# Gathers of a graph network layer: one completion semaphore for each pair of groups

## The chip, the cores and the metric

The kernel runs on one core of a Trainium2 chip. The metric is the device time of one execution in microseconds (us). Several executions are timed, and one further execution is recorded by the hardware profiler.

The engines have these names here: PE multiplies matrices (PEld is its loading of weights), DVE works on vectors, ACT applies functions, POOL is the engine that issues gathers, and SP issues plain transfers. PSUM is the memory that PE writes its results to. Engines tell each other of finished work by semaphores: counters that one raises and others wait on.

## What is computed

The layer works on 12500 nodes with 96 channels and 412500 edges with 4 attributes, sorted by target node `dst`. Cut to what matters:

```python
def mlp(h, W, b, gamma, beta):          # mean and var over all rows
    h = relu(h @ W + b)
    return gamma * (h - mean(h)) * rsqrt(var(h) + 1e-5) + beta

node = mlp(x, W_node, ...)
edge = mlp(edge_attr, W_edge, ...)
message = mlp(concatenate([x[src], x[dst], edge], axis=1), W_msg, ...)
y = x + segment_sum(message, dst) + node
out = layernorm(y)
```

The part that costs is the message of each of the 412500 edges, which needs the row `x[src]` (96 floats, 384 bytes) of an arbitrary node.

## The kernel before

**Units.** 128 edges are a tile, 4 tiles a group (512 edges), 4 groups a block. There are 3223 tiles, 806 groups and 202 blocks.

**Tables.** The product of `x` with the first part of `W_msg` is computed once for each node and put into a table `p_tab` in DRAM (`tables`, L146 to L166); the part for `dst` goes into `q_tab`. The message of an edge is then the row `src` of `p_tab`, plus a small matrix product of its edge attributes and a window of `q_tab`.

**Gathers.** `gather` (L168 to L175) fetches the rows of one group: four indirect transfers, issued by POOL at L172, each of 128 rows. The group's rows land in one tile of SBUF.

**Spilled blocks.** While the tables, the node part (`nodes`, L254 to L284) and the edge statistics (`edge_norm`, L286 to L338) run, POOL already gathers the first 26 blocks ("early" blocks). `blocks` (L177 to L184) gathers 16 tiles into a buffer `stage` (two of these) and SP stores it to DRAM as `spill`. The first three of them gather from `x` itself, since the table isn't there yet. In `edge_norm`, PE L303 multiplies, ACT L307 applies relu, and DVE L309 takes statistics; four PSUM buffers lie between PE and ACT.

**The ring.** Then 21 buffers, each for one group, form a ring (`ring`, tiles named `pg`). POOL fills all 21 (84 gathers) before the main loop.

**The main loop** (in `fast`, L522 to L545) goes over the groups in a fixed order: the 176 late blocks, fetched through the ring, with one early block after every six or seven of them, read back from `spill` as `pb` by SP. For each group k:

- `linear(k + 1)`: PE L464 computes `z` of the next group, four matmuls into one of two PSUM buffers.
- `message(k)`: DVE L475 adds `z` and the gathered rows into `hs`. On a block's third group DVE L478 also builds the places of the targets. On its last group ACT L482 applies relu to all of `hs`, giving `h`.
- `sums(k - 4)`: PE L497 sums `h` of the group before by target node, into `pa`.
- `edges` and `prepare`: once a block, PE L450 and ACT L457 make the next block's edge features `left` by way of `pr`.
- `add`: once a block, DVE L510 and L511 add the sums to `agg` and the second moments to `gram`.
- `load` and `fetch`: once a block, SP loads edge attributes (L408, L410) and the window of `q_tab` (L418) for the block after next.
- `ahead_of`: after each group that came from the ring, POOL issues the four gathers of the group 21 further on, into the buffer that this group's `hs` has just given free.

**What sets the order.** `manual_schedule` keeps the instructions of SP and POOL in the order in which the program writes them from the start, and those of all five engines in the main loop. No scheduler moves anything there.

**Who waits for what.** The framework puts in the waits. It has eight semaphores for POOL's gathers and deals them out in turn. A gather may only be issued when the gather that used the same semaphore last, the one eight before, has landed. The first gather of a group waits, besides, for the DVE instruction that set its buffer free. `hs` at L475 waits for the four gathers of its group, for PE's `z`, and once a block for ACT. An instruction holds one wait of its own; further waits are put ahead of it as separate instructions on the same engine that do nothing else.

Of the kernel before, what the change touches and what calls it, by code (L numbers as in the profile page):

```python
# [26 lines left out]
GT, GE, BG = 4, 512, 4  # L27
NT = -(-E // P)
NG = -(-NT // GT)
# [22 lines left out]
SPILL = 26 * BG  # L52
# [4 lines left out]
CL, CE = 2, 2  # L57
BUSY = 4
J = 8


K, W, ROWS = 4, 128, 12672
# [11 lines left out]
def gnn(ctx, tc, t):  # L74
    nc = tc.nc
# [70 lines left out]
    def tables(work, ps):  # L146
# [3 lines left out]
        for c in range(0, NB, CH):  # L150
# [14 lines left out]
                (nc.scalar if (c // CH + k) % 2 else nc.sync).dma_start(outs[k][:, c:c + CH, :], r[:, :, k, :])  # L165
            yield  # L166

    def gather(g, pg):  # L168
        tab, idx = (t["x"], src_raw) if g < RAW * BG else (p_tab, src)
        for i in range(min(GT, NT - g * GT)):  # L170
            k = g * GT + i
            nc.gpsimd.indirect_dma_start(  # L172
                out=pg[:, i, :], out_offset=None, in_=tab[:, :],
                in_offset=bass.IndirectOffsetOnAxis(ap=idx[:, k:k + 1], axis=0))
        return pg  # L175

    def blocks():  # L177

        for b in range(SPILL // BG):
            pg = ring.tile([P, BG, GT, C], F32, name="stage", bufs=2)  # L180
            for i in range(BG):
                gather(b * BG + i, pg[:, i, :, :])
            nc.sync.dma_start(spill[b], pg.rearrange("p g a c -> p g (a c)"))
            yield  # L184
# [15 lines left out]
    for i in range(NS):  # L200
        k, n = Q * i, C - Q * i
# [84 lines left out]
    def edge_norm():  # L286

        with tc.tile_pool(name="es", bufs=2) as work, tc.tile_pool(name="es1", bufs=1) as one, \
                tc.tile_pool(name="es_ps", bufs=4, space=PSUM) as ps:
            stats = one.tile([P, NS, NBL, 6], F32, name="estats")  # L290
            for b in range(NBL):
                if b % J == 0:
                    yield
                    ea = work.tile([P, J, GE], F32, name="ea")
                    n = min(J, NBL - b)
                    for i in range(NS):
                        nc.sync.dma_start(ea[Q * i:Q * i + 2 * EK, :n, :],
                                          t["ea"][EK * i:EK * (i + 2), b:b + n, :])
                for i in range(NS):
                    k = NS * b + i  # L300
                    if k % 2 == 0:
                        pr = ps.tile([P, 2, GE], F32, name="pr")
                    nc.tensor.matmul(pr[:, k % 2, :], wide[Q * i:Q * i + 2 * EK, :],  # L303
                                     ea[Q * i:Q * i + 2 * EK, b % J, :], start=True, stop=True)
                    if k % 2:
# [34 lines left out]
    def fast(ring):  # L340
        def ahead_of(g):
            return gather(g, ring.tile([P, GT, C], F32, name="pg"))
# [215 lines left out]
    def general():  # L558

        with tc.tile_pool(name="gd", bufs=1, space=DRAM) as gd, tc.tile_pool(name="gfix", bufs=1) as fix, \  # L560
# [108 lines left out]
            with tc.For_i(0, NI, 1) as it:  # L669
                si, di, df, sp = indices(bass.ds(it * IT, IT), IT, P)  # L670
                local = work.tile([C, IG, 6], F32, name="local")
                got = {}
                for g in range(-AHEAD, IG):
                    if g + AHEAD < IG:
                        got[g + AHEAD] = gather(si, di, (g + AHEAD) * GT, GT, P)
                    if g < 0:
                        continue
                    ea = work.tile([EK, GE], F32, name="gea", bufs=3)
                    i = g % BG
                    nc.sync.dma_start(ea, t["ea"][EK * i:EK * (i + 1), bass.ds(it * (IG // BG) + g // BG, 1), :]  # L680
                                      .rearrange("k b e -> k (b e)"))
                    message(g, got.pop(g), ea, df, sp, g * GT, GT, P, local[:, g, :])
                nc.vector.tensor_copy(stats[:, bass.ds(it * IG, IG), :], local)
# [32 lines left out]
    with tc.tile_pool(name="fin", bufs=2) as work, tc.tile_pool(name="fin_ps", bufs=2, space=PSUM) as ps:  # L716
# [14 lines left out]
        for i in range(0, NB, NBY):  # L731
            n = min(NBY, NB - i)
# [55 lines left out]
```

## Time and profile before

| | us |
|---|---|
| timed runs | 5298.15, 5300.56, 5312.70 |
| their median | 5300.56 |
| the profiled execution | 5279.93 |
| its span, first to last instruction | 5278.2 |
| main loop, first to last `hs` | 981.0 to 5222.7 |

| engine | busy us | share of the span |
|---|---|---|
| PE | 3295.6 | 62% |
| PEld | 2492.9 | 47% |
| DVE | 1235.1 | 23% |
| ACT | 1032.9 | 20% |
| POOL | 3073.5 | 58% |

The mean granted clock of PE was 0.652 of full speed. Half-microsecond events count here, so three kinds of view are used. A group of instructions gives a line of the program, the engine, what it writes and reads, how many there were, their busy time and mean, and then the time that the engine stood idle just before them, with what ended it. A view of waits sums these idle times by what ended them: total us, times, longest. A timeline gives start, duration, engine, line and, in brackets, the idle time before and what ended it. "Remote" means that the record shows no nearby instruction whose end would explain the start; "issue" means that nothing the profile shows was waited for.

### The profile page before, as it was taken

What the parts mean: (1) busy time and instruction counts of PE and PEld (TensorE: products, weight loads), DVE (VectorE), ACT (ScalarE), POOL (GpSimd) and SP (SyncE); (2) the same over time, 40 slices, a digit from 0 to 9 for tenths busy, and PEclk for the clock granted to TensorE, in tenths of its full rate; (3) what the DMA queues carried; (4) which work ended last, traced back from release to release, by engine and by line L of the source; (5) the groups of instructions that cost most, each with busy time, mean ns of one, the idle gap of its engine ahead of it and who ended that gap; (6) DMA issues with size and microseconds to landing.
All of it is one profiled execution on the core that took longest, in us unless ns stands there. A gap on an engine that the chain in (4) does not pass through costs nothing. (4 is left out here: it accounts for less than half of the span.)

```text
span 5278.2 us, 46288 instructions
## 1 busy us (share of the span) xinstructions
PE 3295.6 (62%) x16517; PEld 2492.9 (47%) x16517; DVE 1235.1 (23%) x2410; ACT 1032.9 (20%) x804; POOL 3073.5 (58%) x3244
## 2 busy tenths in 40 slices
PE   4366663567666666566666666665666666666667
PEld 3333321445554545445454554554555445455446
DVE  2355652311111111111111111111111111111114
ACT  1144542111111111111111111111111111111112
POOL 6545355264566666666666656666666666665652
PEclk7555555566676676767676666666666666666668
DMA  8333332121122111121111211212111112121213
GB/s 225 98 77 74 67 71 41 26 45 30 40 44 45 44 38 43 44 45 43 39 44 43 45 43 37 44 43 45 43 38 44 43 44 45 37 45 42 45 43 85
DMA packets 190373, 274.29 MB, mean 52 GB/s; under 512 B 121571, under 2 KB 121956, under 8 KB 189126
## 3 DMA queue, kind: packets, MB, share of 16 engines
q0 software_dynamic: 103136, 158.62, 14.8%
q1 hardware_dynamic: 71684, 99.14, 6.8%
q10 hardware_dynamic: 15312, 13.47, 0.9%
q8 instruction: 133, 2.18, 0.2%
q14 instruction: 108, 0.88, 0.1%
HBM read 227.55 MB, written 43.43 MB: 51 GB/s over the span
## 5 line engine op out<-in xcount | busy, mean ns | idle before, releaser
L172 POOL DMA_INDIRECT pg<-p_tab,src x2807 | 2655.1, 946 | 1745.2 <-issue 793.7
L464 PE MATMUL z<-rhs,left 128*128 128x96 f32 x6446 | 1214.6, 338 | 794.8 <-issue 599.8
L464 PEld LDWEIGHTS z<-rhs,left 128*128 128x128 f32 x6446 | 1097.0, 250 | 1096.8 <-issue 785.0
L497 PE MATMUL pa<-h 128*97 128x128 f32 x6446 | 1236.1, 329 | 600.4 <-issue 595.5
L497 PEld LDWEIGHTS pa<-h 128*97 128x97 f32 x6446 | 1010.0, 208 | 685.0 <-issue 682.1
L475 DVE TENSOR_TENSOR hs<-z,pg 128x384 f32<-128x384 f32 x702 | 386.1, 556 | 2906.4 <-remote 1883.3
L457 ACT ACTIVATE left<-pr 127x2048 f32<-127x2048 f32 x202 | 378.3, 1873 | 2481.8 <-remote 1386.2
L303 PE MATMUL pr<-ea,wide 10*128 10x512 f32 x1212 | 403.9, 1075 | 296.0 <-issue 147.1
L172 POOL DMA_INDIRECT stage<-p_tab,src x368 | 353.8, 961 | 349.4 <-DMA spill<-stage 225.7
L450 PE MATMUL pr<-ea,we 7*127 7x512 f32 x1404 | 447.1, 858 | 95.8 <-issue 82.2
L482 ACT ACTIVATE h<-hs 128x1536 f32<-128x1536 f32 x201 | 298.0, 1483 | 1048.4 <-DVE hs L475 596.9
L309 DVE BATCH_NORM_STATS2 estats<-r 128x6 f32<-128x512 f32 x606 | 365.4, 684 | 306.5 <-issue 164.3
L303 PEld LDWEIGHTS pr<-ea,wide 10*128 10x128 f32 x1212 | 195.8, 322 | 502.8 <-issue 293.8
L307 ACT ACTIVATE r<-pr 128x1024 f32<-128x1024 f32 x303 | 293.1, 1024 | 470.3 <-remote 245.4
L450 PEld LDWEIGHTS pr<-ea,we 7*127 7x127 f32 x1404 | 126.4, 239 | 258.6 <-issue 245.0
L510 DVE TENSOR_TENSOR agg<-pa,agg 97x62 f32 x404 | 89.8, 222 | 369.7 <-remote 250.7
L478 DVE TENSOR_TENSOR h<-rel,z 128x496 f32<-128x496 f32 x202 | 133.4, 660 | 0.0
L511 DVE TENSOR_TENSOR gram<-pa,gram 97x388 f32<-97x388 f32 x202 | 111.3, 551 | 0.0
L475 DVE TENSOR_TENSOR hs<-z,pb 128x384 f32<-128x384 f32 x104 | 57.6, 555 | 189.3 <-PE z L464 101.2
L275 PE MATMUL py<-center,xp 96*128 96x96 f32 x196 | 43.4, 424 | 46.6 <-DVE y0s L279 24.6
L157 PE MATMUL pt<-w_msg,xp 96*128 96x192 f32 x196 | 44.3, 398 | 33.5 <-issue 20.2
L275 PEld LDWEIGHTS py<-center,xp 96*128 96x128 f32 x196 | 42.2, 332 | 47.9 <-DVE y0s L279 25.3
(113 smaller groups left out, 536.9 us busy)
## 6 DMA issues: line engine op xcount, KB each, us to landing
pg<-p_tab,src POOLq DMA_INDIRECT x2807
spill<-stage SPq DMA_DIRECT2D x26, 768.0 KB
pb<-spill SPq DMA_DIRECT2D x26, 768.0 KB
ea<-in_ea SPq DMA_DIRECT2D x75, 160.0 KB
rhs<-q_tab SPq DMA_DIRECT2D x202, 46.5 KB
ea<-in_ea SPq DMA_DIRECT2D x352, 20.0 KB
stage<-p_tab,src POOLq DMA_INDIRECT x368
y_d<-y0s SPq DMA_DIRECT2D x12, 384.0 KB
```

Source lines behind the costliest of these rows:

```text
L172: nc.gpsimd.indirect_dma_start(out=pg[:, i, :], out_offset=None, in_=tab[:, :], in_offset=bass.IndirectOffsetOnAxis(ap=idx[:, k:k + 1], ax ...
L303: nc.tensor.matmul(pr[:, k % 2, :], wide[Q * i:Q * i + 2 * EK, :], ea[Q * i:Q * i + 2 * EK, b % J, :], start=True, stop=True)
L307: nc.scalar.activation(r, pr, AF.Relu)
L309: nc.vector.bn_stats(stats[:, (k - o) % NS, (k - o) // NS, :], r[:, 1 - o, :])
L450: nc.tensor.matmul(prs[s][:C + WN, i, :], we[Q * i:Q * i + EK + 2, :], block[s][Q * i:Q * i + EK + 2, :], start=True, stop=True)
L457: nc.scalar.activation(x[:C + WN, :n, :], pr[:C + WN, :n, :], AF.Relu)
L464: nc.tensor.matmul(zs[k][:, i, :], left[s % 2][:KR, g % BG, i * P:(i + 1) * P], rhs[:KR, s % RB, g % BG, :], start=True, stop=True)
L475: nc.vector.tensor_add(hs[:, i, :n, :], z[:, :n, :], pg[:, :n, :])
L478: nc.vector.tensor_tensor(h[:, :, :, C + 1:C + 1 + WN], rel[:, b:b + BG, :].unsqueeze(3).to_broadcast([P, BG, GT, WN]), nodes_of.unsqueeze ...
L482: nc.scalar.activation(h[:, :, :, :C], hs, AF.Relu)
L497: nc.tensor.matmul(pas[s][:, g % BG, :C + 1 + WN], h[:r, i, :C + 1], h[:r, i, :C + 1 + WN], start=i == 0, stop=i == n - 1)
L511: nc.vector.tensor_add(gram[:, :n, :], pa[:, :n, :C + 1], gram[:, :n, :])
```

## The change

Eight further semaphores `own` are set up. For each gather the new function `last(g)` names the group whose last gather others wait for: in a spilled block the block's fourth group, in the ring the second of each two groups (and each of the final two groups by itself). Every gather but that last one raises one of the `own` semaphores on landing, for which nobody waits. It is taken out of the framework's dealing of semaphores and put into a group that counts as done when the last gather is done. So `hs` of the first group of a pair waits for the eighth gather of the pair, and `hs` of the second group has no wait for a gather left; the store of a spilled block waits for one gather instead of all 16 by their semaphores. A last gather still takes the framework's semaphores in turn. What is gathered, into which buffer and in which order stays.

```diff
+OWN = 8
...
+    own = [tc.alloc_semaphore(f"own{i}") for i in range(OWN)]
+
+    def last(g):
+        if g < SPILL:
+            return g // BG * BG + BG - 1
+        return g if g >= NG - 2 else g // 2 * 2 + 1
+
     def gather(g, pg):
         tab, idx = (t["x"], src_raw) if g < RAW * BG else (p_tab, src)
-        for i in range(min(GT, NT - g * GT)):
+        n = min(GT, NT - g * GT)
+        for i in range(n):
             k = g * GT + i
-            nc.gpsimd.indirect_dma_start(
+            dma = nc.gpsimd.indirect_dma_start(
                 out=pg[:, i, :], out_offset=None, in_=tab[:, :],
                 in_offset=bass.IndirectOffsetOnAxis(ap=idx[:, k:k + 1], axis=0))
+            if i < n - 1 or last(g) != g:
+                dma.then_inc(own[last(g) % OWN], 16)
+                tc.no_tile_sem_insts.add(dma.ins.name)
+                tc.add_to_no_dep_group(f"with{last(g)}", dma.ins)
+            else:
+                tc.declare_fence(dma.ins, group=f"with{g}")
         return pg
```

## The prediction

> **What bounds the kernel now.** I read the page first (shares of time, groups), then the waits of the main loop (1200 to 5200 us), then timelines of single stretches. The busy shares name no bound: PE 62%, POOL 58%. The chain that ended last covers only the final 45 us, so it says nothing of the loop. The two groups that matter:
>
> ```profile
> L172 POOL DMA_INDIRECT pg<-p_tab,src x2807 | 2655.1, 946 | 1745.2 <-issue 793.7
> L475 DVE TENSOR_TENSOR hs<-z,pg 128x384 f32<-128x384 f32 x702 | 386.1, 556 | 2906.4 <-remote 1883.3
> ```
>
> A gather occupies POOL 946 ns; with the gap behind it, below, it is 1.25 us, so 16 gathers (one block) take 20.0 us. DVE idles 2906 us ahead of `hs`, mostly for something the page calls remote. What POOL waits for, in the main loop alone (total us, times, longest):
>
> ```profile
> POOL pg L172 <- issue: 733.1, 2302, 2.5
> POOL pg L172 <- DVE hs L475: 616.4, 133, 31.5
> POOL pg L172 <- DVE agg L510: 150.8, 43, 4.8
> POOL pg L172 <- DMA pg<-p_tab,src: 35.1, 115, 0.3
> ```
>
> The second and third rows are waits for a free ring slot (767 us, 176 heads of groups). The last row is what the change touches, a gather waiting for an earlier gather: 115 times, never above 0.3 us. One cycle of the loop shows what really turns it:
>
> ```profile
> 3014.01 1.02 DVE L475 TENSOR_TENSOR hs<-z,pg 128x384 f32<-128x384 f32 x2 [14.15 <-remote]
> 3014.83 0.94 POOL L172 DMA_INDIRECT pg<-p_tab,src  x1 [3.93 <-DVE hs L475]
> ...
> 3023.82 1.86 PE L464 MATMUL z<-rhs,left 128*128 128x96 f32 x8
> ...
> 3033.86 0.95 POOL L172 DMA_INDIRECT pg<-p_tab,src  x1 [0.30 <-issue]
> ...
> 3037.26 0.56 DVE L475 TENSOR_TENSOR hs<-z,pg 128x384 f32<-128x384 f32 x1 [13.77 <-remote]
> 3038.09 0.94 POOL L172 DMA_INDIRECT pg<-p_tab,src  x1 [3.28 <-DVE hs L475]
> ```
>
> POOL restarts, runs 16 gathers until 3034.81, stops with the ring full, and 2.45 us later DVE takes a z that PE had written by 3025.7. So DVE learned of PE's work over 11 us late, and only once POOL had stopped. ACT shows the same in the edge statistics, where it depends on no gather:
>
> ```profile
> 798.07 1.02 ACT L307 ACTIVATE r<-pr 128x1024 f32<-128x1024 f32 x1 [10.18 <-issue]
> ...
> 809.30 1.02 ACT L307 ACTIVATE r<-pr 128x1024 f32<-128x1024 f32 x1 [10.20 <-remote]
> ```
>
> One step takes 11.2 us while POOL gathers; from 896 us on, POOL idle, 0.9 to 1.2 us. My reading: what PE announces reaches the others late while gathers execute, and POOL in turn waits for DVE. The ring is always full, so POOL is paced by DVE, and DVE by that delay. A late block takes 22.53 us on average (175 of them, 3942 us) against the 20.0 us of its gathers.
>
> **The change part by part.** The lists of both programs show the same computing instructions and DMAs in the same order on every engine. What differs is waits. Instructions that do nothing but wait fall from 843 to 160 on POOL, 2311 to 1087 on DVE and 724 to 632 on SP (PE and ACT alike to one; the unused fallback is counted in these).
>
> *Waits of a gather for the gather eight before it.* Now one gather in 8 has such a wait (one in 16 of a spilled block). The price in the trace comes from the start of the run, where the first eight gathers have none:
>
> ```profile
> 10.78 0.95 POOL L172 DMA_INDIRECT stage<-in_x,src_raw  x1 [0.31 <-issue]
> 12.03 0.95 POOL L172 DMA_INDIRECT stage<-in_x,src_raw  x1 [0.30 <-issue]
> 13.28 0.94 POOL L172 DMA_INDIRECT stage<-in_x,src_raw  x1 [0.30 <-issue]
> ```
>
> The seventh and eighth carry no wait, the ninth is the first that does, and all three have the gap of 0.30 us that the main loop has too. A gather lands about 2.2 us after its start and the one eight before started 10 us ago. Taken: 0; bounds 0 and -35 us (the whole last row of POOL's waits). [...]
>
> *The same waits where they do bind.* Only block 0: seven gathers between 15.8 and 28 us have gaps of 0.67 to 1.72 us for an earlier `stage` gather, 3.9 us too much in all; 1.9 us more near 200 us. Both vanish, but block 2 waits 5.3 us at its head for the first spill store and block 3 14.3 us for the table, so POOL would only arrive earlier at these. Taken 0, bounds 0 and -6 us.
>
> *The separate wait ahead of a group's head on POOL.* It stood before the wait for DVE and passes while that one is open: POOL starts 0.26 us after `hs` ends (3014.57 to 3014.83), less than its own gap. Taken 0; at most 176 x 0.27 = -48 us.
>
> *DVE's separate waits before `hs`.* They precede the wait for PE, and the gathers landed long ago, so they are through before z comes. Where DVE isn't waiting they would show as gaps, and don't:
>
> ```profile
> 3051.21 0.55 DVE L511 TENSOR_TENSOR gram<-pa,gram 97x388 f32<-97x388 f32 x1
> 3051.68 0.56 DVE L475 TENSOR_TENSOR hs<-z,pg 128x384 f32<-128x384 f32 x1
> ```
>
> L511 ends at 3051.76 and `hs`, with two such waits, stands right against it. Taken 0. The nearest row for a bound is POOL's 0.27 us of a wake; on the 366 of 758 `hs` in the loop's window that wait neither for remote nor for PE it is at most -99 us.
>
> *The added wait.* The first `hs` of a pair now waits for the second group's gathers too, and behind it on DVE stand `agg`, `gram` and L478, for which PE and POOL wait. Without cover that is four gathers, 5.0 us, for each of 351 pairs: +1755 us. The cover is the full ring: setting each `hs` in the trace against its gathers, the shortest distance is 52 us, and 44 us to the last gather of the pair. For a spilled block the store waited for all 16 gathers before and does now. Taken 0.
>
> *Sum.* 0 on the profiled execution's 5279.93 us (span 5278.2, 1.73 around it). The three timed runs have a median of 5300.56, 20.6 us above it; I forecast that median: **5300 us**, own range 5110 to 5315 by the bounds above (-188 in all) and the spread of the runs.
>
> **The rivals.** All the real ones turn on the delay, whose cause the trace does not name. Its size can be put in one number: how many groups get through between two stops of POOL. With k groups a cycle is 5.0k us of gathers plus a stop of 3.3 us more than a gap (the mean of 3.93 and 3.28, less 0.30). That is 5.83 us a group at k = 4, 5.66 at 5, 5.55 at 6 and 6.10 at 3.
>
> *A. Faster: fewer semaphore waits on POOL and DVE ease the delay.* For it: the change halves the waiting instructions on just the engines involved, and POOL's sequencer, running ahead, is blocked on an earlier gather from about 5 to 11 us into a run of 16; the delay also starts some 7 to 10 us into a run. Against: it lasts until 2 to 3 us after POOL's last gather, long past the end of that blocked phase; after the unbroken 100 gathers before the main loop it lasts 13 to 16 us. That goes with gathers executed, and those stay. Price: k = 5 gives 702 x -0.165 = -116 us (5185), k = 6 -193 us (5107). Gone altogether, a late block falls to its 20.0 us: 175 x -2.53 = -443 us (4858); with early blocks and the loop's 2723 gathers at 1.25 us as the only bound it is about -780 us (4520).
>
> *B. Slower: the delay comes earlier.* Without lane waits POOL's sequencer can queue gathers up to the next head, so nothing separates it from the gathers' execution but the ring; if work queued on POOL is what holds PE's announcements back, it is held from the start of a run, and three groups get through, not four. It decides from the point where the delay starts before the fourth `hs` of a cycle, some 8 us after the restart (3022.35). Price: 702 x +0.275 = +193 us (5493); half of the cycles so, +96 us (5397). For it: 8 us is close to the measured onset. Against: the gathers' pace, which is what the delay follows, was not limited by those waits.
>
> *C. The change does not do what it says*: the waits come back as waits of the pair's last gather. It waits for one 64 gathers before it, 80 us at full pace, so this too costs nothing and ends at 5300.
>
> [...]
>
> **How the numbers follow.** The forecast and C together: 0.40, within 0.3% (16 us, about what a measurement of this kernel can tell from no change). A: 0.35, of it 0.23 down to k = 6 and 0.12 beyond. B: 0.25, as the onset lies so near the edge of the fourth group; 0.20 up to its full price, 0.05 beyond. The range takes in A to k = 6 and B's full price: 5107 to 5493, with 0.17 outside. Since faster and slower hold 0.60 together, the likeliest case's own range stands with the sum.
>
> **What would show it.** Right: L172 still at 1.25 us from start to start; `hs` still behind remote for about 1850 us of the 4000; late blocks at 22.5 us; no DMA wait in front of `hs` longer than before; the gaps of block 0 gone and found again at the heads of blocks 2 and 3. A would show as steps of ACT L307 well under 11.2 us beside gathers and less remote time at `hs`; B as three `hs` between two POOL stops and more, not longer, stops. The forecast is wrong if the remote time moves at all, for every step of it assumes that the delay follows the gathers and not the waits around them.

## The result, and the profile after

22 runs of each kernel, taken in turn, gave 5324.91 us (median; 5304.06 to 5343.17) after and 5299.56 us (5276.95 to 5318.69) before. The ratio is 1.0050, with a 95% interval of 1.0039 to 1.0062. The change made the kernel 25 us slower, where no change was forecast. The profiled execution took 5331.19 us, with a span of 5329.5.

The two groups shown of before, now on the page of the changed kernel (columns as there; L172 has become L181, and L475 L490):

```profile
L181 POOL DMA_INDIRECT pg<-p_tab,src x2807 | 2653.8, 945 | 1782.8 <-issue 822.4
L490 DVE TENSOR_TENSOR hs<-z,pg 128x384 f32<-128x384 f32 x702 | 386.9, 556 | 2773.4 <-remote 1753.7
```

A gather takes what it took, 945 ns for 946. The remote wait ahead of `hs` is about as before. What POOL waits for in the main loop (1200 to 5200 us; total, times, longest):

```profile
POOL pg L181 <- issue: 758.1, 2411, 2.8
POOL pg L181 <- DVE hs L490: 644.1, 124, 30.5
POOL pg L181 <- DVE agg L525: 153.8, 44, 4.8
POOL pg L181 <- DVE h L493: 1.8, 6, 0.3
```

The row for earlier gathers is gone (35.1 us before), and its 115 gaps of 0.3 us stand under issue now: they were the usual gap, as forecast. The waits for a ring slot are 798 us at 168 heads, against 767 us at 176. So POOL's waits in the loop look much the same. (From first to last `hs` the loop takes 4280 us for 4242 in these two profiles, which is most of the 51 us between them; the section on the prediction shows that profiles of other kernels differ as much with either ring.) The first hundred microseconds do not look the same. Three names are needed for them: `pt` is PE's product for the tables, `trow` the copy of it that DVE and ACT make and SP and ACT store, and `rel`, DVE's first work after the tables, takes the base of its block from each edge's target. Timeline of before, two of POOL's early gathers and what follows from them:

```profile
15.78 0.95 POOL L172 DMA_INDIRECT stage<-in_x,src_raw  x1 [0.31 <-DMA stage<-in_x,src_raw]
17.58 0.95 POOL L172 DMA_INDIRECT stage<-in_x,src_raw  x1 [0.86 <-DMA stage<-in_x,src_raw]
...
22.35 0.96 DVE L163 COPY trow<-pt 128x768 f32<-128x768 f32 x1 [1.66 <-issue]
...
45.92 0.01 SPq L183 DMA_DIRECT2D spill<-stage  x1
...
52.51 0.95 POOL L172 DMA_INDIRECT stage<-in_x,src_raw  x1 [5.28 <-DMA spill<-stage]
...
95.54 3.53 DVE L215 TENSOR_TENSOR rel<-dsti,basei 128x3232 f32<-128x3232 int32 x1 [17.82 <-DMA basei<-in_base]
```

And of the changed kernel:

```profile
20.30 0.96 DVE L164 COPY trow<-pt 128x768 f32<-128x768 f32 x1 [3.34 <-PE pt L158]
...
46.96 0.96 DVE L164 COPY trow<-pt 128x768 f32<-128x768 f32 x1 [25.70 <-remote]
...
57.51 0.95 SPq L198 DMA_DIRECT2D spill<-stage  x1
...
66.26 0.95 POOL L181 DMA_INDIRECT stage<-in_x,src_raw  x1 [23.28 <-DMA spill<-stage]
...
88.92 0.96 DVE L164 COPY trow<-pt 128x768 f32<-128x768 f32 x1 [10.04 <-remote]
...
105.29 3.52 DVE L230 TENSOR_TENSOR rel<-dsti,basei 128x3232 f32<-128x3232 int32 x1 [15.41 <-DMA q_tab<-zero]
```

The chain is this. Before, six gathers, five of the first block and one of the second, stood behind gaps of 0.67 to 1.72 us for earlier ones (the view shows one of them). In these pauses PE's results for the tables came through, and DVE made its fourth copy of them at 22.35. After, POOL runs the 32 gathers of the first two blocks without a pause, and the fourth copy waits 25.70 us, until 46.96. SP's store of the first block stands in its queue behind stores of the table and goes out at 57.51 in place of 45.92. The third block's buffer is therefore free only at 66.26, not 52.51. Its 16 gathers then run beside the end of the tables and hold that up too (88.92). `rel` comes 9.75 us later, and the first `hs` at 988.7 us for 981.0.

A second difference stands at the very end, where POOL drains. The view of the program's last line gives instructions with their durations in ns (min/median/max) and start times, first before, then after:

```profile
L784 POOLq DRAIN  x3: 40/113/4145, 5273.2 to 5277.9; - x3
```

```profile
L799 POOLq DRAIN  x3: 40/118/9697, 5318.9 to 5329.2; - x3
```

The first drain of the three takes 9.70 us in place of 4.15, and in both profiles the span ends within 1 us of its end: 5.5 us.

### The profile page after: what moved, and what is told of

It is laid out like the page before. It is cut to its first block, busy times and chain, and to the rows that moved or that the text cites. A ratio compares the mean times of both kernels' runs of the same rounds, so it can differ in the third digit from the quotient of the medians.

```text
span 5329.5 us, 44288 instructions
## 1 busy us (share of the span) xinstructions
PE 3286.0 (62%) x16517; PEld 2512.6 (47%) x16517; DVE 1235.9 (23%) x2410; ACT 1033.8 (19%) x804; POOL 3072.3 (58%) x3244
## 5 line engine op out<-in xcount | busy, mean ns | idle before, releaser
L181 POOL DMA_INDIRECT pg<-p_tab,src x2807 | 2653.8, 945 | 1782.8 <-issue 822.4
L479 PE MATMUL z<-rhs,left 128*128 128x96 f32 x6446 | 1233.5, 338 | 814.3 <-issue 735.2
L479 PEld LDWEIGHTS z<-rhs,left 128*128 128x128 f32 x6446 | 1112.3, 251 | 1104.3 <-issue 929.6
L490 DVE TENSOR_TENSOR hs<-z,pg 128x384 f32<-128x384 f32 x702 | 386.9, 556 | 2773.4 <-remote 1753.7
L181 POOL DMA_INDIRECT stage<-p_tab,src x368 | 353.8, 961 | 344.4 <-DMA spill<-stage 226.1
L465 PE MATMUL pr<-ea,we 7*127 7x512 f32 x1404 | 429.2, 835 | 98.5 <-issue 84.5
L490 DVE TENSOR_TENSOR hs<-z,pb 128x384 f32<-128x384 f32 x104 | 57.5, 555 | 209.4 <-PE z L479 146.1
L181 POOL DMA_INDIRECT stage<-in_x,src_raw x48 | 45.6, 949 | 38.7 <-DMA spill<-stage 23.3
```

Source lines behind the costliest of these rows:

```text
L181: dma = nc.gpsimd.indirect_dma_start(out=pg[:, i, :], out_offset=None, in_=tab[:, :], in_offset=bass.IndirectOffsetOnAxis(ap=idx[:, k:k + ...
L465: nc.tensor.matmul(prs[s][:C + WN, i, :], we[Q * i:Q * i + EK + 2, :], block[s][Q * i:Q * i + EK + 2, :], start=True, stop=True)
L479: nc.tensor.matmul(zs[k][:, i, :], left[s % 2][:KR, g % BG, i * P:(i + 1) * P], rhs[:KR, s % RB, g % BG, :], start=True, stop=True)
L490: nc.vector.tensor_add(hs[:, i, :n, :], z[:, :n, :], pg[:, :n, :])
```

## The experiments

Each was timed in turns with the kernel before; intervals are of 95%. Twelve ran where the kernel before took 5250 to 5300 us. Only ratios within one set compare: in the first and the second set, on one and the same chip, the kernel before took 5258.7 and 5294.2 us, which is further apart than the 25 us in question. The last six ran on two other chips, where it took 4112 to 4115 us, which is a finding of its own. Table of all, with the length of POOL's first final drain:

| kernel | ratio | interval | drain us |
|---|---|---|---|
| ring_only | 1.0009 | 0.9988 to 1.0031 | 6.4 |
| spill_only | 1.0019 | 0.9995 to 1.0044 | 4.9 |
| ring_each | 0.9991 | 0.9968 to 1.0013 | 3.8 |
| ring_four | 1.0008 | 0.9986 to 1.0031 | 9.2 |
| after_again | 1.0038 | 1.0015 to 1.0061 | 9.7 |
| start_kept | 1.0035 | 1.0021 to 1.0049 | 9.7 |
| start_only | 1.0030 | 1.0007 to 1.0053 | 9.1 |
| raw_one | 0.9988 | 0.9973 to 1.0004 | 4.1 |
| ring_again | 1.0026 | 1.0008 to 1.0044 | 6.4 |
| ring_dve | 1.0017 | 0.9994 to 1.0039 | 4.3 |
| ring_pool | 1.0033 | 1.0014 to 1.0052 | 9.4 |
| null | 1.0010 | 0.9989 to 1.0032 | 4.1 |
| on the other chips: | | | |
| kept_again | 0.9982 | 0.9973 to 0.9991 | 9.7 |
| ring_third | 1.0003 | 0.9994 to 1.0012 | 6.4 |
| after_third | 0.9985 | 0.9976 to 0.9994 | 9.7 |
| each_kept | 0.9982 | 0.9973 to 0.9991 | 7.4 |
| spill_8 | 1.0758 | 1.0742 to 1.0775 | 4.1 |
| spill_14 | 1.0471 | 1.0455 to 1.0487 | 4.1 |

**First set: ring or spilled blocks, pairs or groups.** Theory 1: the loss comes from the main loop, through the thinner waits on POOL and DVE. Theory 2: it comes from the start, as just told. Theory 3: it comes from the pair's wait.

ring_only:

```diff
+            if g < SPILL:
+                continue
             if i < n - 1 or last(g) != g:
```

> The change in the ring alone; the spilled blocks are gathered as before. The changed kernel took 1.005 times the time before. Theory 1 (the loss comes from the main loop: with the waits of POOL and DVE thinned out the delay of PE's announcements grows or falls differently): about 1.004 to 1.005, main loop some 20 us longer than the 4242 us of before. Theory 2 (the loss comes ahead of the loop: the first spilled blocks are gathered faster and delay the tables and the node part, which ended 10 to 19 us later in the changed kernel's profile): 1.000 with the first hs near 981 us. Theory 3 (the pair's wait): as theory 1.

spill_only:

```diff
+            if g >= SPILL:
+                continue
             if i < n - 1 or last(g) != g:
```

> The change in the 26 spilled blocks alone; the ring is as before. Theory 1 (main loop): 1.000, and the first hs near 981 us. Theory 2 (start): 1.004 to 1.005 would need more than the 8 us by which the first hs came later in the changed kernel's profile; 1.001 to 1.002 if those 8 us are all of it.

ring_each, which is ring_only and:

```diff
-        return g if g >= NG - 2 else g // 2 * 2 + 1
+        return g
```

> Ring alone, and each group keeps its own last gather with a semaphore (last(g) = g), so that hs waits for its own four gathers as before, by one wait in place of four; gathers of a group have one wait for an earlier gather in place of four. Theory 1 (thinner waits on POOL and DVE): most of the loss stays, 1.003 to 1.005. Theory 3 (hs of a pair's first group waits for the second group's gathers): 1.000.

ring_four, which is ring_only and:

```diff
-        return g if g >= NG - 2 else g // 2 * 2 + 1
+        return g if g >= NG - 2 else g // 4 * 4 + 3
```

> Ring alone, with one semaphore for four groups (last(g) = the fourth of each four), so one hs in four waits, for 16 gathers. Theory 3 (waiting for gathers of later groups): clearly more loss than with pairs, 1.01 or more, with DMA pg waits ahead of hs in the view of waits. Theory 1: 1.004 to 1.006, hardly more than with pairs, since 7 of 8 waits are already gone there.

No part alone gave the 1.005. `rel` came at 103.4 us in spill_only, and at 92.1 to 94.0 us in the three with the old spilled blocks. The first `hs` was at 971.5 us against 958.8 to 966.8. So the start's loss of about 9 us at `rel` is bound to the spilled blocks, as theory 2 says. Theory 3 falls: ring_four lets one `hs` wait for 16 gathers and costs no more than ring_only; DVE waits for no gather in its profile's main loop. In the changed kernel's trace the shortest time from a pair's last gather to its first `hs` is 55 us.

**Second set: the start alone, and all but the start.** after_again is the changed kernel itself.

> The changed kernel once more, on one chip together with the parts of it. Theory 2, extended (the loss is the start, 8 to 10 us until the table is done, plus something in the ring that the ring alone did not show): 1.003 to 1.005, with rel (the first DVE work on the places) near 104 us where the kernels with the old spilled blocks have it at 92 to 95 us. If it is within 1.002, the 1.005 measured first depends on the chip.

start_kept:

```diff
+            if g < RAW * BG:
+                continue
             if i < n - 1 or last(g) != g:
```

> The changed kernel, but the first three spilled blocks, which are gathered from x while the tables are computed, keep all waits for the gather eight before. Theory 2: the start is as before, rel near 94 us and the first hs some 9 us earlier than in after_again, and the ratio 0.002 below that of after_again. Theory 1 (only the ring matters): as after_again, with rel near 94 us but no gain.

start_only:

```diff
+            if g >= RAW * BG:
+                continue
             if i < n - 1 or last(g) != g:
```

> The change in the first three spilled blocks alone; the other 23 and the ring are as before. Theory 2: rel near 104 us, first hs 8 to 10 us later than in the kernels with the old start, 1.002. Theory 1: 1.000.

raw_one, made from the kernel before:

```diff
-RAW = 3
+RAW = 1
...
-                if i in (2, 4):
+                if i == 2:
...
-                if i in (1, 5, 10):
+                if i in (1, 3, 5, 10):
```

> The kernel before, but only one spilled block, not three, is gathered from x before the tables are done (RAW = 1); blocks 1 and 2 are gathered from p_tab when it stands, and need no conversion in the loop. If gathers beside the tables hold the tables up by delaying what PE announces (theory 2's mechanism), the tables end earlier than the 78 us of before, rel comes 10 to 20 us earlier, and POOL, which has some 100 us to spare ahead of the loop, loses nothing: 0.995 to 0.998. If the tables are bound by their loads and stores: no earlier end, 1.000 or more.

What delays the start is shown. In start_only 45 gathers of 3223 are changed, and `rel` moves to 105.5 us, the third block's head waits 23.96 us for the store, and the first `hs` comes at 991.9 us. In start_kept, which changes all others, `rel` is at 95.7 and the first `hs` at 971.2. after_again has 104.9 and 988.8. The same two lines in start_only and start_kept, from their timelines:

```profile
47.75 0.96 DVE L164 COPY trow<-pt 128x768 f32<-128x768 f32 x1 [25.73 <-remote]
...
66.89 0.94 POOL L181 DMA_INDIRECT stage<-in_x,src_raw  x1 [23.96 <-DMA spill<-stage]
```

```profile
19.94 0.96 DVE L164 COPY trow<-pt 128x768 f32<-128x768 f32 x1 [1.66 <-PE pt L158]
...
53.23 0.94 POOL L181 DMA_INDIRECT stage<-in_x,src_raw  x1 [5.01 <-DMA spill<-stage]
```

raw_one bears the mechanism out from the other side. Without gathers of the second and third block beside the tables, their last product starts at 61.8 us, not 77.5, and `rel` at 78.1, not 95.5. But the gain was given back: these blocks' gathers now run beside the node part and the edge statistics. The first step of the statistics came 13 us later (286.3 us against 273.1), the last 31 us later (973.8 against 942.7), and the first `hs` at 1011.9. The loop then took 4212 us, 30 less than in before's profile; two blocks fewer are converted in it, and whether that is all of the 30 us was not tested. The total, 0.9988, cannot be told from no change; my 0.995 to 0.998 took POOL to have 100 us to spare, and overlooked whom its gathers would disturb in that time.

The parts do not simply add up. start_only's 16 us (0.0030 of 5294) are about the start's loss and 4.9 us of drain, but less the drain its 1.0021 has 1 within its interval of 0.0023. start_kept should have been 0.002 below after_again and is 0.0003 below it, with intervals of 0.0014 and 0.0023. So the total times neither show nor exclude that the start's delay reaches the end in full; the delay itself is read from the profiles. start_kept still lost 0.0035, or 18.5 us, of which the drain is 5.5. The other 13 us would have to stand in the ring or in the other spilled blocks, which the third set examines.

**Third set: the rest.** ring_again is ring_only.

> The change in the ring alone, once more, beside its two halves. It gave 1.0009 (0.9988 to 1.0031), while the whole change without the first three blocks gave 1.0035 (1.0021 to 1.0049). If the ring costs something: 1.002 to 1.003. If it costs nothing and the remaining 23 spilled blocks do, or chance: 1.000 to 1.001.

ring_dve is ring_only and:

```diff
-                dma.then_inc(own[last(g) % OWN], 16)
-                tc.no_tile_sem_insts.add(dma.ins.name)
                 tc.add_to_no_dep_group(f"with{last(g)}", dma.ins)
```

> Ring alone, and only DVE's side of it: hs waits for the last gather of a pair as in the change, but every gather keeps the framework's semaphores, so POOL has all waits for the gather eight before. Theory 1a (POOL without those waits queues ahead and the delay falls worse): 1.000. Theory 1b (fewer waits on DVE change when it takes what): as ring_again. No effect of either: 1.000.

ring_pool is ring_only with 84 semaphores, four for each ring slot, and DVE's waits for them:

```diff
-                dma.then_inc(own[last(g) % OWN], 16)
+                q = g % RING * 4 + i
+                counts[q] += 16
+                rose.setdefault(g, []).append((q, counts[q]))
+                dma.then_inc(own[q], 16)
...
+                if g in rose:
+                    for q, v in rose[g]:
+                        nc.vector.wait_ge(own[q], v)
                 nc.vector.tensor_add(hs[:, i, :n, :], z[:, :n, :], pg[:, :n, :])
```

> Ring alone, and only POOL's side: seven of eight gathers of a pair have semaphores of their own outside the framework, so POOL has one wait for an earlier gather in eight, but DVE waits for each gather of the group by itself (eight waits for a pair, as before). Theory 1a: as ring_again or more, 1.002 to 1.003. Theory 1b: 1.000.

null, made from the kernel before:

```diff
+    spare = const.tile([P, 1], F32, name="spare_v")
+    for i in range(16):
+        nc.vector.memset(spare, 0.0)
     zero = const.tile([64, C], F32, name="zero")
```

> The kernel before with 16 small memsets of one column on DVE after the tables, which nobody reads; DVE waits for loads there. They cost nothing on the path, and only move what follows by some instructions. Every theory expects 1.000; what it gives beyond its interval is what a shift without meaning makes of this kernel, and differences between the others under that are not read.

ring_pool's ratio is clear of 1, but 5.2 of its 17 us are its drain. Less its longer drain, each kernel that changes the ring alone would stand between 0.999 and 1.002, and the mean of the six is 1.001; null stands there too. Two of them, ring_again (1.0022) and ring_pool (1.0023), stay just clear of 1 by their own intervals. So these runs neither show nor exclude a loss of one or two thousandths in the ring. start_kept, less its drain, keeps 1.0025, with an interval of 0.0014 to either side. Whether that is the other 23 spilled blocks, something small in the ring, or partly chance, stays open.

**Fourth set: other chips.** kept_again is start_kept, ring_third is ring_only, and the other two are the kernel before with fewer spilled blocks.

> start_kept once more (the change without the first three spilled blocks). So far the loss is made up of about 9 us until the tables are done (absent here) and 5.5 us in POOL's last drain (9.7 us in place of 4.1, present here); a rest of some 10 us is open. If the rest is real, in the ring or the 23 other spilled blocks: 1.003 again. If it was chance: 1.001, which is the drain alone.

> ring_only for the third time (1.0009 and 1.0026 so far), its drain 2.3 us longer than before's. Rest real and in the ring: 1.002 to 1.003. Rest in the other spilled blocks, or chance: 1.000 to 1.001.

```diff
-SPILL = 26 * BG
+SPILL = 8 * BG
```

> The kernel before with 8 spilled blocks, not 26. Tests the reason on which everything rests, that what PE announces comes late while POOL gathers: then a gather ahead of the loop is not free, but holds the edge statistics up by nearly its own time. 18 blocks fewer take some 360 us of gathers from beside the statistics, in which these get only 360 / 11.2 = 32 steps done; at about 1.2 us a step without gathers that is 320 us saved. In the loop 18 blocks cost 22.53 us in place of 11.46, 199 us more. Sum -120 us, 0.977. If gathers beside the statistics were free, the loop's 199 us would be lost in full: 1.038.

```diff
-SPILL = 26 * BG
+SPILL = 14 * BG
```

> The same with 14 spilled blocks. By the same reckoning 12 x (20 x (1 - 1.2 / 11.2) - 11.07) = -81 us, 0.985; if gathers beside the statistics were free, +133 us, 1.025.

All of these expectations rested on a kernel of 5250 to 5300 us. Here it took 4114.55, and the waits show what is different (changed kernel, after_third, 700 to 4000 us):

```profile
DVE hs L490 <- DMA pg<-p_tab,src: 2212.8, 279, 12.0
...
POOL pg L181 <- issue: 797.0, 2615, 0.3
```

There is no remote wait at `hs` any more, and none in the same stretch of ring_third or of spill_8, whose gathers all wait as in the kernel before. `hs` waits for gathers; in this stretch POOL never waits longer than its gap of 0.3 us. And the step of the edge statistics beside running gathers, 11.2 us in the trace of before:

```profile
399.61 1.02 ACT L322 ACTIVATE r<-pr 128x1024 f32<-128x1024 f32 x1 [0.16 <-DVE estats L324]
399.63 0.94 POOL L181 DMA_INDIRECT stage<-p_tab,src  x1 [0.30 <-issue]
400.80 1.02 ACT L322 ACTIVATE r<-pr 128x1024 f32<-128x1024 f32 x1 [0.16 <-DVE estats L324]
```

It is 1.19 us. What PE announces is not late on these chips, although gathers have the same pace of 1.25 us. PE's granted clock was higher too, 0.70 to 0.75 in these runs for some 0.65 in the others, but PE's mean for one matmul of `z` was 341 ns in kept_again's profile for 338 in before's, so the clock does not make a step ten times as long. Here POOL is busy or in its usual gap almost from start to end, and a gather moved into the loop costs most of its time: spill_8 loses 313.7 us for 18 blocks (17.4 each), spill_14 194.2 us for 12 (16.2 each), against 20.0 us of gathers in a block. In spill_8's profile POOL stands idle for 320.2 us ahead of the first `hs`, with the ring full. These two could not test the delay, since there was none. Whether fewer spilled blocks gain where announcements are late was not run.

The sign of the change itself does turn: start_kept, slower by 0.35% on the first chips, is faster by 0.18% here. ring_third, with the old spilled blocks, shows what the waits among spilled gathers cost where POOL is the bound (POOL's waits, 100 to 620 us):

```profile
POOL stage L181 <- DMA stage<-p_tab,src: 17.6, 18, 2.6
```

That row is absent in after_third. The first `hs` comes at 629.8 us in ring_third, at 618.4 in kept_again on the same chip and at 619.1 in after_third.

**Last two runs**, on another chip of this second kind. after_third is the changed kernel.

> The whole change once more, on whatever chip comes. Where the kernel before takes 5250 to 5300 us (PE's announcements late under gathers): 1.004 to 1.005. Where it takes 4114 us, as on the chip of kept_again: there POOL never stops and every gather that comes earlier shortens the run; the waits among spilled gathers cost some 11 us there, the first three blocks' waits up to 5 more, the drain gives 5.5 back: 0.997 to 0.998.

each_kept is start_kept with `return g` in the ring, as in ring_each.

> The change with the first three spilled blocks as before and, in the ring, one semaphore for each group and not for two. ring_each gave 0.9991 with a drain of 3.8 us, start_kept 1.0035 with a drain of 9.7 us. On a chip with late announcements 0.999 to 1.002, better than the change by what start and drain cost; on the other 0.997 to 0.998.

The whole change gains 5.6 us here (0.9985): some 11 us by the first `hs`, less 5.5 us in the drain, which comes to about as much. each_kept gives 0.9982 and cannot be told from it. It did not run where announcements are late, so whether it beats both kernels there is not known.

## Why the prediction was wrong

Point by point, by its own steps:

- **What bounds the kernel.** Right for the chips where the forecast applies: PE's results reach DVE, ACT and SP late while gathers run. What the trace of one execution could not tell is that this belongs to the chip (or to whatever else differed between these sets of runs), not to the kernel: elsewhere the step is 1.19 us, not 11.2. All sets with the delay were run before those without, so chip and time of the run are not told apart.
- **Waits for the gather eight before, in the main loop: 0.** Right. The gap stayed at 0.30 us and the row of 35.1 us went into issue. No time came back to POOL's pace: from start to start a gather takes 1.25 us in both profiles.
- **The same waits where they do bind: 0, bounds 0 and -6 us.** This step failed, with its sign. I wrote that "POOL would only arrive earlier at these" heads, and priced what POOL gains. The waits had a second effect: they paced the first block, and PE's results came through in the pauses. Without them the store of block 0 is 11.6 us later, block 2's gathers 13.8 us, `rel` 9.75 us. The gaps were to be found again at the heads of blocks 2 and 3; instead block 2's head went from 5.28 to 23.28 us, four times what the gaps had been, and block 3's from 14.27 to 10.63. The first `hs` came 8 us later in the two profiles first compared, and 5 to 21 us later between kernels of one set. start_only and start_kept show it from both sides, and on the chips where PE's results aren't late it is gone: `rel` is at 83.5 us in after_third, at 82.8 and 82.4 in ring_third and kept_again, which have the old start. My rival B named this mechanism, "held from the start of a run", and I priced it for the loop alone, where POOL's pace was never limited by these waits. (That POOL's sequencer gets further ahead without them is seen in the changed kernel's profile: it passed the wait ahead of block 6 at 158.07 us, ten gathers before that block's first one started at 172.16. In before's main loop it was never more than six ahead.) I had the fact that makes the start different, gaps of 0.67 to 1.72 us, in the same text. (They are six gaps with 4.2 us too much, not seven with 3.9.)
- **Separate waits on POOL and DVE: 0.** Not contradicted. ring_dve, with DVE's waits thinned alone, gave 1.0017 (0.9994 to 1.0039).
- **The added wait of a pair: 0.** Right for the reason given where announcements are late: the ring is full and the cover is 55 us. Elsewhere it came out right by luck: the ring is empty and `hs` waits for gathers, 2213 us between 700 and 4000 us in after_third, but there POOL is the bound, and ring_third is at 1.0003.
- **The end of the program.** No step of the sum looked at it, so its term was nothing without a reason. POOL's drain there went from 4.15 to 9.70 us, 5.5 of the 25 us.

Start and drain make 15 us of the 25, if the 9.75 us at `rel` reach the end. The other 10, with an interval of some 6 us to either side from the 22 runs, are open: the first `hs` within one set differed by more than `rel` did, and start_kept keeps 13 us after its drain, but no experiment pins a place.

Rival A, a relief of the delay, did not come. DVE's remote waits between 1200 and 5200 us, before:

```profile
DVE hs L475 <- remote: 1859.3, 190, 17.2
DVE agg L510 <- remote: 238.6, 37, 12.0
DVE hs L475 <- DMA pg<-p_tab,src: 129.2, 22, 14.0
```

and after:

```profile
DVE hs L490 <- remote: 1690.9, 183, 16.4
DVE agg L525 <- remote: 387.6, 48, 12.1
```

The remote time at `hs` fell by 168 us and that at `agg` rose by 149: time moved from one waiter to another. The third row of before, which the prediction did not show, has no counterpart after, but it is no wait for a gather in the sense of the change: the gathers of a group had landed over 40 us before its `hs` throughout. By the same views, all idle time ahead of `hs` and `agg` together is 3281 us before and 3273 after. The loop, 4242 us before, took 4280 in the one profile after, and 4271 in after_again, 4266 in start_kept and 4276 in start_only, whose ring is the old one. Over the first three sets, profiles of the old ring gave 4235 to 4276 us (raw_one aside) and those of a new one 4239 to 4271, so the loop differs as much between runs as between rings. Rival B's sign in the loop, more stops of POOL, did not come either: there were 168 for 176.

## What to carry to other kernels

A wait that costs its own engine a microsecond may be worth more than that to another engine: before taking it away, ask what happens in the pause, not only what the waiter gains. Price a change in each stage by that stage's limit, the prologue and the final drain included: here the first 100 us, in which three queues hang on each other, and a drain of under 10 us showed clearer differences than a loop of over 4200. And where a profile shows a delay that no instruction explains, look at it on more than one chip before tuning for it: here the same edit slows the kernel by 0.4 to 0.5% with the delay and speeds it up by 0.15% without it.

## What the runs showed of the hardware that was not expected

- While POOL issued gathers, PE's results became visible to ACT, DVE and SP late on some chips: a step of 11.2 us in the edge statistics, where others have 1.19 us with gathers at the same pace of 1.25 us; SP's loads of the `q_tab` window have 1539.5 us of remote waits in before's main loop. The kernel before took 5250 to 5300 us on the former and 4112 to 4115 on the latter. What differs between them is not known.
- POOL's first drain at the end takes between 3.8 and 9.7 us, the same within 0.01 us in every profile of one program, on both kinds of chip (9.695 to 9.697 us in three profiles of the changed kernel, 6.428 to 6.430 in three of ring_only). It does not follow the number of POOL's instructions (start_only has before's number, and 9.1 us for 4.1), nor the number of gathers that raise a semaphore of their own: 45 of them give 9.1 us (start_only), 390 give 4.9 (spill_only), and 2455 give 6.4 or 9.4 (ring_only, ring_pool). What sets it was not found.
